# A hybrid of scan, linear attention and ternary feed-forward on one core: the bias behind a one-column copy, weights' sums moved, a shifted instruction stream and a third output bank

## The chip, the cores and the metric

The kernel runs on one core of a Trainium2 chip. The core has engines that each work through their own list of instructions in turn: PE (TensorE, matrix products, with PEld for its weight loads), DVE (VectorE), ACT (ScalarE), POOL (GpSimd), and SP (SyncE), which issues most transfers. They wait for one another through semaphores. The metric is the device time of one execution in microseconds (us). Before the change it is 1060.16 us, the median of three runs (1059.4 to 1060.26). One execution was also recorded by the hardware profiler; all views of the profile are of that one.

## The reference

The input x has two sequences of 2048 rows with 256 columns. Four layers are added to it, each on the layer-normalised x: a gated scan, a feed-forward with ternary weights, a higher-order linear attention, and the same feed-forward again.

```python
x = x + _L0_attn_a_ref(_layernorm(x), gamma, w_qkva)      # q * scan(sigmoid(a), kv) of an RMS-normed x
x = x + _L0_ffn_ref(_layernorm(x), W1, b1, W2, b2)
x = x + _L0_attn_b_ref(_layernorm(x), W_q, W_k, W_v, W_o)
x = x + _L0_ffn_ref(_layernorm(x), W1, b1, W2, b2)
...
# feed-forward
h = jnp.einsum('bsd,fd->bsf', x, _ternary(W1)) + b1       # 1024 hidden columns
h = jax.nn.gelu(h, approximate=False)
out = jnp.einsum('bsf,df->bsd', h, _ternary(W2)) + b2
...
# attention: 16 heads of 64, states S_K, C_QV, G carried from row to row
k_C = jnp.einsum('bhk,bhkv->bhv', k_t, C_QV)
G = G + k_t[..., :, None] * k_C[..., None, :]
S_K = S_K + k_t[..., :, None] * k_t[..., None, :]
C_QV = C_QV + q_t[..., :, None] * v_t[..., None, :]
o_t = jnp.einsum('bhk,bhkv->bhv', q_t, jnp.einsum('bhkj,bhjv->bhkv', S_K, C_QV) - G)
```

`_ternary(W)` rounds W over the mean of its magnitudes to -1, 0 or 1.

## The kernel before

All of x stays in SBUF (`x_sb`), as 32 chunks of 128 rows. Four chunks are a block; the list `blocks` has eight, those of the two sequences in turn. The work has three stages, each in a scope of its own: the **front** (scan and first feed-forward, 0 to 227 us), **attention** (227 to about 945 us) and the **last feed-forward** (to the end). In each scope the order of the instructions on PE, DVE, ACT and POOL is written out by hand: an engine runs its instructions in the order in which the Python code emits them. SP's transfers are issued in their order too.

**Front** (`front`). It starts with units of the scan (`s_` statistics, `r_` normalised rows, `t_` turned rows, `q_` the scan itself, `a_` the sum into x) and then loops over the eight blocks. For block i it emits `ffn_in` (eight steps, one for each 128 hidden columns: four matmuls into one bank `ph`, one GELU on ACT; after every second step `Hidden.split` makes a high half `hh` on ACT and the rest `hl` on DVE) and `ffn_out` (eight steps of eight matmuls into two banks `o`, then DVE adds them to x). For i = 0 to 3 the scan of a later unit runs between the steps of `ffn_in` (`scan_steps`, whose products can be cut into m parts of the 512 columns). The rows of the feed-forward to come are prepared by `fs_` (statistics: bn_stats on DVE, four small operations on POOL that give `rs` and `nb`), `fq_` (normalised rows `xn` on ACT, squares turned by DVE, out to DRAM and back by SP) and `fe_` (`halves_end`: the conversion `xh` on ACT, the rest `xl` on DVE). `ffn_bias(g0)` (L548 to L551) adds b2 to a whole block of x on POOL; it must come before DVE's sum of that block. Here it stands at the end of the loop's body, for the block after.

**The seam.** Attention multiplies by Strassen's scheme with seven products (`Seven`), so it needs sums of the weights' quarters. `weights_kv(w, t)` (L465 to L472) makes them with four POOL operations of 128 x 512. Here `later` has three of them, for wk, wv and wq, emitted at i = 4, 5 and 6. Attention's first pair of chunks (one of each sequence) is prepared by `then`: `attention_stats` (four small POOL operations at the end), `attention_rows` (`xn` on ACT, squares, SP's round trip) and `attention_turned` (the copy `xnT_first`). They stand after step 4 of `ffn_in` of i = 6, in `ffn_out` of i = 6, and after `ffn_in` of i = 7.

**Attention** (`attention`). At first `pair_sums(0)` makes the four sums `S` of the first pair on POOL, `norm_stats` the statistics of pair 1 (DVE, then POOL), and the products of k, q and v of pair 0 follow, with `norm_rows` of pair 1 on ACT in the middle. `Seven.go(i)` emits product i of seven on PE and its eviction or sum: 1, 5, 6 and 4 are copied by ACT, 0, 7 and 3 added by DVE; the banks X and Z of k and of v are the same two (ring `oT`). The tables `in_two` and `first_in_two` say which products are cut into two matmul calls (the second one for pair 0 alone). Then the loop over 32 steps s (`NS`, one chunk each): `inter`, `products`, `intra`, `evict`, `update`, `outward`, and transfers through DRAM that turn keys and units (`keys_out`, `units_out`, `turn_rows`, `turn_end`). In its last four steps the class `Last` starts the last feed-forward's block 0: it brings the ternary weights back from DRAM in four transfers each, issued by ACT (`weights`, `part`: `w1r_back` from s = 28, `w2r_back` from s = 29, the latter with `part(4)`), and fills PE with steps of `ffn_in`.

**Last feed-forward.** For each block: `ffn_in`, from step 4 on the statistics of block i + 3, `halves_end` of block i + 2, rows and squares of block i + 3, `ffn_out` with the store, and then `ffn_bias` of block i + 1. In the last block `ffn_out` (L523 to L546) runs all eight steps for chunks 0 to 2 and then all eight for chunk 3, whose sum goes into the second half of the bank that holds chunk 2.

Of the kernel before, what the change touches and what calls it, by code (L numbers as in the profile page):

```python
# [23 lines left out]
P = 128  # L24
# [20 lines left out]
def kernel(  # L45
# [477 lines left out]
    def ffn_out(g0, hid, store=False, tag="ps"):  # L523

        banks = [bank([P, 2, D], f"o{g0}_{i}", tag) for i in range(2)]
        if store and g0 == blocks[-1]:
            order = [(f, range(BC - 1)) for f in range(NF)] + [(f, range(BC - 1, BC)) for f in range(NF)]
        else:
            order = [(f, range(BC)) for f in range(NF)]
        for f, cs in order:  # L530
            for c in cs:
                to = banks[c // 2][:, c % 2, :]
                for k, h in enumerate((hid.hi, hid.lo)):
                    nc.tensor.matmul(  # L534
                        to, lhsT=h[f // 2][:, f % 2, c * P : (c + 1) * P], rhs=w2r[:, f, :],
                        start=(f == 0 and k == 0 and c % 2 == 0), stop=(f == NF - 1 and k == 1),
                        skip_group_check=True,
                    )
                m = 1 if len(cs) < BC and c > 1 else 2
                if f == NF - 1 and (c % 2 == 1 or m == 1):  # L540
                    g = g0 + c + 1 - m
                    xs = x_sb[:, g : g + m, :]
                    nc.vector.tensor_tensor(xs, xs, banks[c // 2][:, c % 2 + 1 - m : c % 2 + 1, :], ALU.add)  # L543
                    if store:
                        nc.sync.dma_start(out=rows(of, g, m), in_=xs)
            yield  # L546

    def ffn_bias(g0):  # L548

        xs = x_sb[:, g0 : g0 + BC, :]  # L550
        nc.gpsimd.tensor_tensor(xs, xs, b2_sb.unsqueeze(1).to_broadcast([P, BC, D]), ALU.add)  # L551

# [7 lines left out]
    def front(scan_pool, ffn_pool, tern_pool, then, later):  # L560
# [112 lines left out]
        for i in range(NB):  # L673
            u, g0 = i + 5, blocks[i]
            more, scans = i + 1 < NB, u < len(units)
            hid, staged = hidden(ffn_pool, g0)
            steps = ffn_in(g0, fn.pop(i), hid, staged)
            if i == 0:
                ffn_bias(g0)
            if scans:  # L680
                ys[u] = []
                products = scan_steps(scan_pool, units[u][0], xnT[u], last[units[u][0] // CPB], ys[u], 2 if i > 1 else 1)
                for j in range(4):
                    run(products, 1)
                    run(steps, 1)
                    if i == 0 and j == 0:
                        a_(4)
                        fq_(1)
                run(products)
                if i == 3:  # L690
                    fq_(5, scan_pool, "xn")
            else:
                run(steps, 4)
                if i == 4:
                    fs_(7)
                if i == NB - 2:
                    then[0]()
            if u + 1 < len(units):
                s_(u + 1)
            if i == 0:  # L700
                fs_(2)
            run(steps)
            if u + 1 < len(units):
                r_(u + 1)
            if i == 5:
                wq = const.tile([P, ND, H * DK], FP, tag="wq", name="wq")
                nc.sync.dma_start(out=wq, in_=w_q.rearrange("(c p) e -> p c e", p=P))
            if not more:
                wo = const.tile([P, NPR, D], FP, tag="wo", name="wo")
                nc.sync.dma_start(out=wo, in_=w_o.rearrange("(c p) e -> p c e", p=P))  # L710
                then[2]()

            steps = ffn_out(g0, hid, tag="out")
            if i > 3 and i - 4 < len(later):
                later[i - 4]()
            if i == 2:
                ffn_weights_away()
            if scans:
                fe_(i + 1)
                run(steps, 2)  # L720
                a_(u)
                run(steps, 3)
                if u + 1 < len(units):
                    t_(u + 1)
            if i < 3:
                fq_(i + 2)
                fs_(i + 3)
                if i == 2:
                    fs_(6)
            elif i == 3:  # L730
                fq_(6)
                fe_(5)
            elif i + 2 < NB:
                fe_(i + 2)
                if i + 3 < NB:
                    fq_(i + 3)
            if i == NB - 2:
                then[1]()
            run(steps)
            if more:  # L740
                ffn_bias(blocks[i + 1])

# [6 lines left out]
    def attention(keep, pool, state, last):  # L751
# [22 lines left out]
            pairs[n] = x, S  # L774

        in_two = {"kN": (1, 5, 3), "vN": (1, 5)}
        first_in_two = {"kN": (2, 4, 6, 7), "vN": ()}

        class Seven:

# [220 lines left out]

        NS = len(steps)
        pair_sums(0)
        stats = norm_stats(norm_pool, pair(1), bias=True)
        k, q, v = Seven(0, "kN", "oT"), Seven(0, "qT", "uT"), Seven(0, "vN", "oT")
        k.go(2, 1, 0, 5)
# [21 lines left out]
        for s in range(NS):  # L1028
# [27 lines left out]
            if s < NS - 2:  # L1056
                last.part()
            elif s == NS - 2:
                last.part(None)
            if s >= 3:  # L1060
                outward(s - 3, 1)
            intra(s, "S", "kN", "p1", "uT")
# [7 lines left out]
            if not more:  # L1070
                if first:
                    units_out(s)
                    turn_rows(s, "uN")
                else:
                    evict(s - 2, "oT", dve)
                last.begin(first)
                fill = last.fill
                fill(1)
                if first:
                    fill(1)  # L1080
                    last.his()
                    evict(s - 2, "oT", act)
                else:
                    units(s)
                    fill(2)
                    last.his()
            elif first:
                if s != 2:
                    k = Seven(n + 1, "kN", "uT" if s > 0 else "oT")
                    k.go(2)  # L1090
                k.go(1)
                if s >= 2:
                    evict(s - 2, "oT")
                else:
                    units_out(s)
                    turn_rows(s, "uN")
                k.go(0, 5)
                if s == 0:
                    k.go(6)
            else:  # L1100
                if s >= 2:
                    evict(s - 2, "oT", dve)
                if s > 1 or not more:
                    units_end(s - 1)
                units_out(s)
                turn_rows(s, "uN")
                if n + 2 < CPB:
                    raw = norm_squares(pool, pair(n + 2), [xn], 2, "xraw", 1)
                if s > 1:
                    q.go(2)  # L1110
                    v.go(2)
                for part in (q, v) if s > 1 else (v, q):
                    part.go(1)
                if s == NS - 3:
                    last.part()
                q.go(0, 5)
                v.go(0, 5)
                if s == 1:
                    units_end(s - 1)
                q.go(6)  # L1120
                v.go(6)
# [60 lines left out]
            if s == NS - 3:  # L1182
                last.part(None)
                last.weights(False)
                last.part(4)
            if s >= 2:
                outward(s - 2, 0)
        last.out()
# [24 lines left out]
    def pair(n):  # L1213
        return [b * CPB + n for b in range(B)]
# [116 lines left out]
    with (  # L1331
        tc.tile_pool(name="scan", bufs=2) as scan_pool,
        tc.tile_pool(name="ffn1", bufs=2) as ffn_pool,
        tc.tile_pool(name="tern", bufs=2) as tern_pool,
        tc.manual_schedule(engines=by_hand),
    ):

        warm = bank([P, P], "warm")
        for _ in range(12):
            nc.tensor.matmul(warm, lhsT=ones, rhs=ones, start=True, stop=True)  # L1340
        nc.scalar.activation(table, ones[:, :1], AF.Sigmoid)
        front(
            scan_pool, ffn_pool, tern_pool, (attention_stats, attention_rows, attention_turned),
            [lambda: weights_kv(wk, wk_t), lambda: weights_kv(wv, wv_t), lambda: weights_kv(wq, wq_t)],
        )
    front_ctx.close()

# [1 line left out]
    with tc.tile_pool(name="keep", bufs=3) as keep_pool:  # L1349
# [10 lines left out]
        with tc.tile_pool(name="ffn2", bufs=1) as ffn_pool, tc.manual_schedule(engines=by_hand):  # L1360
            two_rings()
            steps, rhs, raws = last.outs, last.turns, {}
            for i, g0 in enumerate(blocks):
                more, ahead = i + 1 < len(blocks), i + 3 < len(blocks)
                if i > 0:
# [6 lines left out]
                    steps = ffn_out(g0, hid, True, "out")  # L1372
                    if i + 2 < len(blocks):
                        rhs[i + 2] = halves_end(raws.pop(i + 2), rows_room(ffn_pool, blocks[i + 2], bufs=2))
                if ahead:
                    if i > 0:
                        last.rows(blocks[i + 3])
                    raws[i + 3] = norm_squares(ffn_pool, chunks(blocks[i + 3]), last.xn, 1)
                run(steps)
                if more:  # L1380
                    ffn_bias(blocks[i + 1])


# [35 lines left out]
```

## Time and profile before

| what | us |
|---|---|
| three runs | 1059.4, 1060.26, 1060.16 |
| profiled execution | 1059.29 |
| its span, first to last instruction | 1057.1 |
| PE busy | 1046.6 |
| DVE, ACT, POOL busy | 732.1, 613.3, 185.2 |
| `ffn_out` of the front's last block | 219.7 to 227.2 |
| POOL's `S` of pair 0 | 227.5 to 229.3 |
| PE's last matmul | 1053.62 |

In a timeline a row has start, time, engine, line, operation, the tiles written and read, the shape and the count; in brackets stands the idle time of the engine before it and what ended that. In the list of waits a row says who waited for whom: us in total, times, the longest. "issue" is idle time that no engine ended. PE's matmuls overlap, so a group's time runs to the modelled end of its last one; the time between the starts of two groups is the better measure. The span is shorter than the time of the execution by 2.2 us.

### The profile page before, as it was taken

The numbers are of one execution on the slowest core, as the hardware profiler recorded it, in microseconds if no ns is written. First come the engines' busy times: TensorE is split into PE (matmuls) and PEld (weight loads), VectorE is DVE, ScalarE is ACT, GpSimd is POOL, SyncE is SP. The second block draws the span as 40 slices with busy tenths as digits, with TensorE's granted clock in tenths as the row PEclk, the third lists the DMA queues.
The fourth block names the chain that finished last, engine by engine and source line by source line (L and its number), as shares of the span: only waits on it lengthen the run. The fifth ranks groups of instructions, "written<-read, shape, count | busy, mean of one in ns | idle before, by whom it ended". The sixth has DMA issues, their size and how long they took to land.

```text
span 1057.1 us, 43926 instructions
## 1 busy us (share of the span) xinstructions
PE 1046.6 (99%) x20136; PEld 847.1 (80%) x20136; DVE 732.1 (69%) x1047; ACT 613.3 (58%) x813; POOL 185.2 (18%) x282
## 2 busy tenths in 40 slices
PE   9999999999999999999999999999999999999998
PEld 7567889887778887878778788787877877888987
DVE  7987788846675765766666666666675766668973
ACT  4567779754645555445554455545545554668884
POOL 3433243831101001011010110101101010014230
PEclk9999999999999999999999999999999999999999
DMA  9231112203432433423324243242332435123321
GB/s 313 81 120 41 41 41 80 80 28 114 143 124 90 133 102 105 142 81 124 121 85 143 86 139 111 75 142 103 122 122 83 141 105 170 35 101 101 120 81 40
DMA packets 80826, 111.24 MB, mean 105 GB/s; under 512 B 8321, under 2 KB 66561, under 8 KB 80385
## 3 DMA queue, kind: packets, MB, share of 16 engines
q1 hardware_dynamic: 79024, 106.07, 30.3%
q8 instruction: 157, 2.57, 1.0%
q10 hardware_dynamic: 1584, 2.36, 0.8%
q14 instruction: 29, 0.23, 0.1%
q0 software_dynamic: 32, 0.00, 0.0%
HBM read 57.81 MB, written 50.59 MB: 103 GB/s over the span
## 4 chain that ended last, share of the span: by engine, by line
PE 87%; DVE 5%; DMA 2%; ACT 2%; issue 2%; POOL 1%; SPq 0%; ACTq 0%; DVEq 0%; POOLq 0%
PE hy L962 10%; PE o L534 7%; PE h L512 7%; PE hkN_X L827 6%; PE hp L882 6%; PE hqT_X L819 6%; PE hvN_X L827 6%; PE pq L368 4%; PE pq L390 3%; PE huT L899 3%; PE hoT L899 3%; PE huT L913 3%; PE hS L939 3%; PE hoT L913 3%; PE hM L939 3%; PE hqT_Z L819 3%
## 5 line engine op out<-in xcount | busy, mean ns | idle before, releaser
L888 DVE TENSOR_TENSOR p<-hp,mask 128x512 f32<-128x512 f32 x128 | 82.3, 684 | 83.4 <-PE hp L882 83.4
L962 PE MATMUL hy<-wo,oT 128*128 128x256 f32 x512 | 124.0, 386 | 0.0
L962 PEld LDWEIGHTS hy<-wo,oT 128*128 128x128 f32 x512 | 93.5, 190 | 19.1 <-issue 6.9
L773 POOL TENSOR_TENSOR S<-xnT 128x128 f32<-128x128 f32 x30 | 13.9, 463 | 514.8 <-ACT xnT L312 514.8
L497 DVE TENSOR_TENSOR hl<-h,hh 128x1024 fp32r<-128x1024 f32 x60 | 83.0, 1395 | 28.3 <-ACT hh L491 28.1
L518 ACT ACTIVATE h<-h,b_sb 128x512 f32<-128x512 f32 x120 | 77.6, 682 | 42.9 <-PE h L512 33.7
L924 ACT COPY uT<-huT 128x512 f32<-128x512 f32 x32 | 18.7, 585 | 123.3 <-PE huT L913 123.3
L194 ACT ACTIVATE xn<-x_sb,nb,rs 128x256 f32<-128x256 f32 x124 | 65.2, 592 | 18.3 <-POOL nb L180 18.3
L951 DVE TENSOR_TENSOR S<-S,hS 128x512 f32<-128x512 f32 x60 | 41.3, 688 | 42.3 <-PE hS L939 39.3
L259 DVE STREAM_TRANSPOSE squN<-uT 128x1024 f32<-128x1024 f32 x31 | 63.8, 2058 | 5.5 <-ACT uT L926 5.1
L259 DVE STREAM_TRANSPOSE sqkT<-kN 128x1024 f32<-128x1024 f32 x32 | 65.8, 2058 | 1.3 <-ACT kN L859 1.2
L981 ACT COPY kT<-rawkT 128x1024 f32<-128x1024 f32 x32 | 66.7, 2085 | 0.0
L981 ACT COPY uN<-rawuN 128x1024 f32<-128x1024 f32 x31 | 64.7, 2086 | 3.2 <-DMA w2r_back<-dw2r 2.9
L491 ACT CAST hh<-h 128x1024 fp32r<-128x1024 f32 x60 | 63.1, 1051 | 1.9
L534 PE MATMUL o<-w2r,hl 128*128 128x256 f32 x256 | 61.1, 281 | 0.4 <-DVE hl L497 0.2
L534 PE MATMUL o<-w2r_back,hh 128*128 128x256 f32 x248 | 60.6, 284 | 0.9 <-DVE x_sb L543 0.9
L534 PE MATMUL o<-w2r_back,hl 128*128 128x256 f32 x248 | 60.6, 283 | 0.9 <-DVE hl L497 0.7
L534 PE MATMUL o<-w2r,hh 128*128 128x256 f32 x256 | 61.3, 282 | 0.0
L859 ACT COPY vN<-hvN_X 128x512 f32<-128x512 f32 x16 | 9.4, 586 | 78.8 <-PE hvN_X L827 78.8
L162 DVE BATCH_NORM_STATS2 st<-x_sb 128x6 f32<-128x256 f32 x128 | 51.3, 401 | 2.3 <-DMA x_sb<-in_x_dram 2.3
L833 DVE TENSOR_TENSOR kN<-kN,hkN_Y 128x512 f32<-128x512 f32 x16 | 11.0, 688 | 60.2 <-ACT kN L842 60.2
L534 PEld LDWEIGHTS o<-w2r,hl 128*128 128x128 f32 x256 | 48.2, 188 | 1.5 <-DVE hl L497 1.0
(227 smaller groups left out, 2583.0 us busy)
## 6 DMA issues: line engine op xcount, KB each, us to landing
dsqkT<-sqkT SPq DMA_DIRECT2D x32, 512.0 KB, 3.8
rawkT<-dsqkT SPq DMA_DIRECT2D x128, 128.0 KB, 2.9
dsquN<-squN SPq DMA_DIRECT2D x31, 512.0 KB, 3.2
rawuN<-dsquN SPq DMA_DIRECT2D x124, 128.0 KB, 3.0
dsqxn<-sqxn SPq DMA_DIRECT2D x14, 512.0 KB, 2.7
rawxn<-dsqxn SPq DMA_DIRECT2D x56, 128.0 KB, 2.9
out_dram<-x_sb SPq DMA_DIRECT2D x15, 256.0 KB, 3.0
x_sb<-in_x_dram SPq DMA_DIRECT2D x7, 512.0 KB, 9.0
```

What stands on the lines that cost most here:

```text
L194: nc.scalar.activation(xn[:, c, :], x_sb[:, g, :], AF.Identity, bias=nb[:, c : c + 1], scale=rs[:, c : c + 1],)
L259: nc.vector.transpose(to, src)
L497: nc.vector.tensor_tensor(self.lo[a], h, self.hi[a], ALU.subtract)
L512: nc.tensor.matmul(ph, lhsT=w1r[:, d, f * P : (f + 1) * P], rhs=r[:, d, :], start=(d == 0 and k == 0), stop=(d == ND - 1 and k == 1),)
L518: nc.scalar.activation(h[:, f % 2, :], ph, AF.Gelu, bias=b1_sb[:, f : f + 1])
L534: nc.tensor.matmul(to, lhsT=h[f // 2][:, f % 2, c * P : (c + 1) * P], rhs=w2r[:, f, :], start=(f == 0 and k == 0 and c % 2 == 0), stop=(f ...
L819: nc.tensor.matmul(to[:, j, :], lhsT=self.B[i][:, j * P : (j + 1) * P], rhs=self.A[i], start=(new and j == 0), stop=True, skip_group_check ...
L827: nc.tensor.matmul(to[:, cols], lhsT=self.A[i], rhs=self.B[i][:, cols], start=(new and j == 0), stop=True, skip_group_check=True,)
L882: nc.tensor.matmul(banks[h][halves[c], p, :], lhsT=d[s][left][halves[h], p, halves[c]], rhs=d[s]["qT"][halves[h], p, halves[c]], start=Tru ...
L888: nc.vector.tensor_tensor(d[s][nm][:, h], banks[h], mask8, ALU.mult)
L962: nc.tensor.matmul(py, lhsT=d[s]["oT"][:, p, :], rhs=wo[:, p, :], start=(p == 0), stop=(p == NPR - 1),)
L981: act(t, d[s]["r" + nm].rearrange("p t q -> p q t"))
```

## The change

- **Bias.** `ffn_bias` begins with a copy of one column of `b2_sb` onto itself on DVE. POOL's bias reads that column, so it can't start until DVE, in its order, has come to the copy. The calls move: in the front from the end of the body to just after `fe_` of the same block (for i = 4 to 6 after the steps named in the diff), in the last feed-forward to just after `halves_end`.
- **Order of the front.** `fe_(5)` goes from i = 3 to i = 4, `fe_(6)` stays at i = 4, `fe_(7)` goes from i = 5 to i = 6; `fs_(7)` and `fq_(7)` go from i = 4 to i = 5. `later` is `weights_kv(wk)` alone, at i = 6 after the bias; `attention_stats` follows it there; `attention_rows` stands after step 2 of `ffn_in` of i = 7. `weights_kv` of wq and wv go into attention, between `pair_sums(0)` and the statistics of pair 1.
- **Instruction stream.** The scan's products at i = 1 are cut in two (`2 if i > 0`), and the products 2, 4 and 6 of v of pair 0 too. Each cut adds a matmul call; a call with 32-bit operands is two weight loads and two matmuls in the trace.
- **Weight back.** `part(4)` becomes `part(2)`; at s = 30 one part is issued where before all that was left would have been, and one more after the eviction and the outgoing squares of that step.
- **Last bank.** Chunk 3 of the last block sums into a third bank of the ring `ps`, with `start` on its first matmul.

```diff
--- before.py
+++ after.py
@@ -525,28 +525,31 @@
         banks = [bank([P, 2, D], f"o{g0}_{i}", tag) for i in range(2)]
         if store and g0 == blocks[-1]:
             order = [(f, range(BC - 1)) for f in range(NF)] + [(f, range(BC - 1, BC)) for f in range(NF)]
+            banks.append(bank([P, 2, D], f"o{g0}_2"))
         else:
             order = [(f, range(BC)) for f in range(NF)]
         for f, cs in order:
             for c in cs:
-                to = banks[c // 2][:, c % 2, :]
+                at = c // 2 if len(cs) > 1 else 2
+                to = banks[at][:, c % 2, :]
                 for k, h in enumerate((hid.hi, hid.lo)):
                     nc.tensor.matmul(
                         to, lhsT=h[f // 2][:, f % 2, c * P : (c + 1) * P], rhs=w2r[:, f, :],
-                        start=(f == 0 and k == 0 and c % 2 == 0), stop=(f == NF - 1 and k == 1),
+                        start=(f == 0 and k == 0 and (c % 2 == 0 or at == 2)), stop=(f == NF - 1 and k == 1),
                         skip_group_check=True,
                     )
                 m = 1 if len(cs) < BC and c > 1 else 2
                 if f == NF - 1 and (c % 2 == 1 or m == 1):
                     g = g0 + c + 1 - m
                     xs = x_sb[:, g : g + m, :]
-                    nc.vector.tensor_tensor(xs, xs, banks[c // 2][:, c % 2 + 1 - m : c % 2 + 1, :], ALU.add)
+                    nc.vector.tensor_tensor(xs, xs, banks[at][:, c % 2 + 1 - m : c % 2 + 1, :], ALU.add)
                     if store:
                         nc.sync.dma_start(out=rows(of, g, m), in_=xs)
             yield
 
     def ffn_bias(g0):
 
+        nc.vector.tensor_copy(b2_sb[:, :1], b2_sb[:, :1])
         xs = x_sb[:, g0 : g0 + BC, :]
         nc.gpsimd.tensor_tensor(xs, xs, b2_sb.unsqueeze(1).to_broadcast([P, BC, D]), ALU.add)
 
@@ -679,7 +682,7 @@
                 ffn_bias(g0)
             if scans:
                 ys[u] = []
-                products = scan_steps(scan_pool, units[u][0], xnT[u], last[units[u][0] // CPB], ys[u], 2 if i > 1 else 1)
+                products = scan_steps(scan_pool, units[u][0], xnT[u], last[units[u][0] // CPB], ys[u], 2 if i > 0 else 1)
                 for j in range(4):
                     run(products, 1)
                     run(steps, 1)
@@ -690,11 +693,12 @@
                 if i == 3:
                     fq_(5, scan_pool, "xn")
             else:
+                if i == 5:
+                    fs_(7)
+                elif not more:
+                    run(steps, 2)
+                    then[1]()
                 run(steps, 4)
-                if i == 4:
-                    fs_(7)
-                if i == NB - 2:
-                    then[0]()
             if u + 1 < len(units):
                 s_(u + 1)
             if i == 0:
@@ -711,12 +715,13 @@
                 then[2]()
 
             steps = ffn_out(g0, hid, tag="out")
-            if i > 3 and i - 4 < len(later):
-                later[i - 4]()
             if i == 2:
                 ffn_weights_away()
+            if i == 4:
+                fe_(5)
             if scans:
                 fe_(i + 1)
+                ffn_bias(blocks[i + 1])
                 run(steps, 2)
                 a_(u)
                 run(steps, 3)
@@ -729,16 +734,18 @@
                     fs_(6)
             elif i == 3:
                 fq_(6)
-                fe_(5)
-            elif i + 2 < NB:
-                fe_(i + 2)
-                if i + 3 < NB:
-                    fq_(i + 3)
-            if i == NB - 2:
-                then[1]()
+            elif i == 4:
+                fe_(6)
+                ffn_bias(blocks[i + 1])
+            elif i == 5:
+                ffn_bias(blocks[i + 1])
+                fq_(7)
+            elif i == 6:
+                fe_(7)
+                ffn_bias(blocks[i + 1])
+                later()
+                then[0]()
             run(steps)
-            if more:
-                ffn_bias(blocks[i + 1])
 
 
 
@@ -774,7 +781,7 @@
             pairs[n] = x, S
 
         in_two = {"kN": (1, 5, 3), "vN": (1, 5)}
-        first_in_two = {"kN": (2, 4, 6, 7), "vN": ()}
+        first_in_two = {"kN": (2, 4, 6, 7), "vN": (2, 4, 6)}
 
         class Seven:
 
@@ -1001,6 +1008,8 @@
 
         NS = len(steps)
         pair_sums(0)
+        weights_kv(wq, wq_t)
+        weights_kv(wv, wv_t)
         stats = norm_stats(norm_pool, pair(1), bias=True)
         k, q, v = Seven(0, "kN", "oT"), Seven(0, "qT", "uT"), Seven(0, "vN", "oT")
         k.go(2, 1, 0, 5)
@@ -1056,7 +1065,7 @@
             if s < NS - 2:
                 last.part()
             elif s == NS - 2:
-                last.part(None)
+                last.part()
             if s >= 3:
                 outward(s - 3, 1)
             intra(s, "S", "kN", "p1", "uT")
@@ -1073,6 +1082,8 @@
                     turn_rows(s, "uN")
                 else:
                     evict(s - 2, "oT", dve)
+                if first:
+                    last.part()
                 last.begin(first)
                 fill = last.fill
                 fill(1)
@@ -1182,7 +1193,7 @@
             if s == NS - 3:
                 last.part(None)
                 last.weights(False)
-                last.part(4)
+                last.part(2)
             if s >= 2:
                 outward(s - 2, 0)
         last.out()
@@ -1341,7 +1352,7 @@
         nc.scalar.activation(table, ones[:, :1], AF.Sigmoid)
         front(
             scan_pool, ffn_pool, tern_pool, (attention_stats, attention_rows, attention_turned),
-            [lambda: weights_kv(wk, wk_t), lambda: weights_kv(wv, wv_t), lambda: weights_kv(wq, wq_t)],
+            lambda: weights_kv(wk, wk_t),
         )
     front_ctx.close()
 
@@ -1372,13 +1383,13 @@
                     steps = ffn_out(g0, hid, True, "out")
                     if i + 2 < len(blocks):
                         rhs[i + 2] = halves_end(raws.pop(i + 2), rows_room(ffn_pool, blocks[i + 2], bufs=2))
+                if more:
+                    ffn_bias(blocks[i + 1])
                 if ahead:
                     if i > 0:
                         last.rows(blocks[i + 3])
                     raws[i + 3] = norm_squares(ffn_pool, chunks(blocks[i + 3]), last.xn, 1)
                 run(steps)
-                if more:
-                    ffn_bias(blocks[i + 1])
 
 
 # ---- launch: one core; inputs and outputs as the reference has them ----
```

## Prediction

> **What bounds the kernel now.** I read the page first, then the waits of the matmul engine (PE), then the timelines of PE, ACT, DVE and POOL where PE stands still.
>
> ```profile
> span 1057.1 us, 43926 instructions
> ...
> PE 1046.6 (99%) x20136; PEld 847.1 (80%) x20136; DVE 732.1 (69%) x1047; ACT 613.3 (58%) x813; POOL 185.2 (18%) x282
> ```
>
> PE is busy from 1.05 to 1053.9 us. A time is won only where PE stands still, and lost wherever an instruction before PE comes late. POOL's 18% says nothing of its order: it works its list strictly in turn, and so does ACT. The two views that decide this case are POOL's and ACT's timelines around the seam between the front and attention:
>
> ```profile
> 209.47 1.29 POOL L469 TENSOR_TENSOR wq_t<-wq 128x512 f32<-128x512 f32 x1
> ...
> 214.59 2.41 POOL L551 TENSOR_TENSOR x_sb<-x_sb,b_sb 128x1024 f32<-128x1024 f32 x1
> 227.50 0.46 POOL L773 TENSOR_TENSOR S<-xnT_first 128x128 f32<-128x128 f32 x1 [10.50 <-PE o L534]
> ...
> 229.41 0.22 POOL L174 TENSOR_SCALAR rs<-mv 128x2 f32<-128x2 f32 x1
> ...
> 230.78 0.23 POOL L180 TENSOR_SCALAR nb<-nb 128x2 f32<-128x2 f32 x1
> ```
> ```profile
> 215.03 1.05 ACT L491 CAST hh<-h 128x1024 fp32r<-128x1024 f32 x1
> ...
> 236.64 1.09 ACT L194 ACTIVATE xn<-x_sb,nb,rs 128x256 f32<-128x256 f32 x2
> 238.09 0.58 ACT L859 COPY kN<-hkN_X 128x512 f32<-128x512 f32 x1 [0.36 <-PE hkN_X L827]
> ```
>
> The reader is to see that S (pair_sums) waits 10.5 us for the last matmul of the front, that pair 1's `rs` and `nb` stand behind it although DVE had their statistics by 207.4, and that ACT's `xn` of pair 1 (236.64) stands ahead of the eviction at 238.09. PE's `hvN_X` begins at 238.78, just after that eviction's end (238.67), in the bank it frees.
>
> PE's own stops, in the places the change touches:
>
> ```profile
> PE o L534 <- DVE x_sb L543: 0.9, 1, 0.9
> PE o L534 <- DVE hl L497: 0.9, 3, 0.4
> PE hoT L913 <- issue: 0.8, 1, 0.8
> ```
> ```profile
> 370.48 1.49 PE L913 MATMUL hoT<-p,vN 64*64 64x64 f32 x64
> ```
> ```profile
> 718.56 1.11 PE L913 MATMUL hoT<-p,vN 64*64 64x64 f32 x64
> ```
>
> The last two are the same 64 matmuls in two rounds: one takes 0.38 us longer, and no engine released it.
>
> **Last bank (gain 1.1).** PE starts a matmul at 1050.51 and the next at 1051.73, where 0.12 is usual: chunk 3 shares its bank with chunk 2, which DVE is still reading. A third bank takes that wait away. The new bank comes from the ring of six whose oldest tile was read long before. The end follows PE, DVE's last add and SP's last store, all 1.1 us earlier.
>
> **Bias held (gain 1.9).** In the last feed-forward the bias (2.41 us) meets DVE's subtractions: two `hl` take 3.49 us at 1011.90 against 1.23 each alone, `xl` 3.56 at 959.54. PE loses 0.23 at 967.6, 0.50 at 972.0 and 0.54 at 1014.3; I take 1.1 of the 1.27, since the statistics stay in front of one `hl`. In the front PE loses 0.36, 0.25 and 0.26 at 177.7, 193.2 and 195.4, where POOL works on weights and bias; I take 0.8. Between 0 and 2.1 in all. The new one-column copy is at most like the 0.17 us of DVE's smallest rows, 16 times, beside 31% idle: nothing.
>
> **The 65 instructions (gain 2.4).** Splitting `pq` at i = 1 and vN's products 2, 4 and 6 adds 15 matmul calls; the time of the halves is that of the whole (216 against 429 to 432 ns from start to start): nothing by itself. But it moves every later instruction in PE's instruction stream. The page has 157 instruction packets of 16 KB on queue 8: 256 instructions each. Counting PE's instructions, the stops in `hoT` are all at the same place modulo 256, so they are waits for the next packet. One round of attention is nine packets long, and the stop comes back in nine rounds with 0.16 to 0.33 us, 2.4 us in sum. The packet that is late left at 368.92, behind the 512 KB of `dsqkT` that ran from 367.0 to 368.8. Moved by 65 instructions it is asked for about 0.47 us earlier, at some 366.8, 0.2 us ahead of that burst. The other eight packets of a round keep their distances. So I take all 2.4; 0 if the margin of 0.2 fails, and 2.4 lost if another packet falls into a burst.
>
> **Weight back in three parts (gain 1.2).** At 886.0 to 889.4 ACT issues four parts in a row, and PE then loses 0.82 at 893.9 to a late instruction packet, and 1.5 more in five smaller stops from 866 to 908. With two parts there and two in the next step the transfers are shorter by half at that point, and all packets shift by 65. I take about half of the 2.3, from 0 to 2.
>
> **Front's order: the first loss (6.5).** `fe_`, `fq_` and `fs_` move by one block; for blocks 5 and 6 the halves are ready with ffn_in's need to within 0.1 us (two conversions of 2.35 on ACT, then 2.27 on DVE): nothing. The point is block 6. There POOL gets, in this order: the bias of block 7, held until `xl` of block 7 is done; weights_kv(wk); the four operations of attention_stats. On the clock of before: ACT ends the last `hh` of block 6 at 207.88, converts `xh` (2.25) to 210.15, DVE's `xl` (2.27) ends 212.4. Bias 2.41: 214.9. The four weights operations are 5.12 (209.47 to 214.59) plus one meeting with DVE's `hl` (1.2): 221.2. Then 1.6 (229.41 to 231.0): `nb` at 222.8. ACT now has attention_rows after two steps of ffn_in(7), so it asks for `nb` at 216.1 and stands 6.7 us, with the GELUs of steps 2 to 7 queued behind it. PE finishes ffn_in from free banks at 219.7, uses the first two steps' hidden until 221.8 and waits. ACT: `xn` 1.1, two GELUs 1.25, `hh` 1.05 to 226.2; DVE's `hl` to 227.4. PE has stood 5.6 us, then follows ACT's 2.25 us for each 1.87 of its own: ffn_out ends at 233.7 instead of 227.2. Between 5.1 (no meeting with DVE) and 7.5 (a second one). SP's round trip of the first rows (7.7 us from `xn` to landing in this trace) ends at 231.7, inside that. The wo load behind it on SP is needed 50 us later.
>
> **Attention's start: the second loss (4.2).** After S (end 229.3) POOL now does weights_kv(wq) and (wv), 8 x 1.28 = 10.2 us, then the 1.6 us for pair 1: `nb` at 241.2 instead of 231.0. ACT stands at 236.6 until then, `xn` 1.1, the kN eviction 0.58: 242.95. PE's `hvN_X` starts at 243.0 instead of 238.78. wq_t and wv_t themselves are in time (230.7 for a use at 234.2; 235.8 for 240.6). Bounds 3.9 to 4.5.
>
> **PE's clock (1.75).** No row has PE idle for 5 us in the middle. At the end the granted clock falls to 0.50 by 1055.9, 2.0 us after the last matmul; at the start 24 warm-up matmuls are 213 ns apart instead of 109 for about 3.5 us. So each of the two idles may cost up to 1.75 us, or nothing: 0 to 3.5. I take one of the two. The Trainium skill, "TensorE: Matmul & The Clock Gate", Part 1, would have it that one idle window of about 3.4 us must pass whole, in a free-running grid; by that the longer idle halves the clock more often than the shorter, an estimate of 1.5 us in place of 1.75. The row asks for less idleness than the page.
>
> **Sum.** Gains 1.1 + 1.9 + 2.4 + 1.2 = 6.6; losses 6.5 + 4.2 + 1.75 = 12.45; +5.9. The profiled execution took 1059.29 us (span 1057.1 and 2.2 around it), so 1065.2; the median of before, 1060.16, lies 0.9 above it, so 1066.0. This case's own range: losses 9.0 to 15.5 against gains 7.5 to 3.5, that is 1061.5 to 1072.
>
> **Rivals.** (1) Faster: both `nb` are ready when ACT asks (216.1 and 236.6), because the small operations get past the weights on POOL. Then only the gains stay: 1053.6. It decides from the point where the two waits sum to less than 6.6 us. Against it stands the row of 229.41, which waited 22 us behind S. (2) The bias isn't held: the copy waits for nothing that matters. Then POOL is done with block 6 before ACT asks, the first loss and the 1.9 of the hold go, and 1.1 + 2.4 + 1.2 against 4.2 and 0.9 of clock leave 1060.5. DVE's rows are in turn everywhere, which speaks against. (3) The new place of the packets is no better: instead of 2.4 + 1.2 won, 2.4 lost: 1072. The burst is only 0.2 us away, but the nine rounds agree to 0.03.
>
> **Chances.** Forecast 0.60; rival 1 0.22; rival 2 0.10; rival 3 0.08. A change under 0.2% (2.1 us) can hardly be told from none. Faster: 0.22 and half of rival 2, 0.27; same 0.06; slower 0.67. The range takes in rival 1 and nearly rival 3: 1053.5 to 1071.5.
>
> **What will show it.** First loss: ACT's `xn` of pair 0 idle some 6 us before it with POOL's `nb` named, PE's `o` of block 7 stopped. Second: ACT's `xn` of pair 1 near its predecessor plus 4 us, PE stopped before `hvN_X`. Gains: `hoT` at 1.11 in every round, no 0.9 us wait in the last block, `xl` at 2.3 throughout. I am wrong if ACT doesn't wait for either `nb`.

## The result, and the profile after

The changed kernel takes 1066.89 us (median of six runs, 1066.52 to 1069.37) against 1059.38 us for the kernel before (six runs, 1058.19 to 1060.26). The ratio is 1.0077, with a 95% interval of 1.0065 to 1.009: about 7.5 to 8 us slower. The profiled execution took 1066.52 us, the one of before 1059.29.

Where the time went is read from PE's starts: the same matmul is looked up in both traces, and the differences are taken from place to place.

| stretch | after - before, us |
|---|---|
| front, to the first product of `ffn_out` of block 7 | -1.22 |
| `ffn_out` of block 7, to the first product of attention | +7.32 |
| from there to `hvN_X` | +3.97 |
| from there to the first `hy` of chunk 0 | +1.61 |
| loop, chunk 3 to chunk 26 | -3.36 |
| end of the loop, chunk 26 to chunk 29 | +2.34 |
| last feed-forward, to `ffn_out` of block 7 | -2.09 |
| last bank | -1.22 |

The sum is +7.35. The page's first lines:

```profile
span 1064.8 us, 44002 instructions
...
PE 1045.1 (98%) x20166; PEld 853.6 (80%) x20166; DVE 718.4 (67%) x1063; ACT 612.2 (57%) x813; POOL 180.1 (17%) x282
```

PE's busy time is 1.5 us less than before and the span 7.7 us longer: it is PE's idle time that grew. The list of PE's waits (us, times, the longest) names the places:

```profile
PE o L536 <- ACT hh L491: 4.4, 1, 4.4
PE hvN_X L834 <- ACT kN L866: 3.8, 1, 3.8
PE hS L946 <- issue: 1.4, 1, 1.4
PE hoT L920 <- issue: 1.0, 1, 1.0
PE o L536 <- DVE hl L497: 0.7, 1, 0.7
PE hp L889 <- issue: 0.6, 1, 0.6
```

The first, second and fifth are the seam. POOL's and ACT's timelines show what stands behind them:

```profile
211.19 2.41 POOL L554 TENSOR_TENSOR x_sb<-x_sb,b_sb 128x1024 f32<-128x1024 f32 x1 [14.78 <-issue]
213.55 1.30 POOL L469 TENSOR_TENSOR wk_t<-wk 128x512 f32<-128x512 f32 x1
214.93 2.36 POOL L470 TENSOR_TENSOR wk_t<-wk,wk_t 128x512 f32<-128x512 f32 x1
...
221.26 0.24 POOL L180 TENSOR_SCALAR nb<-nb 128x2 f32<-128x2 f32 x1
233.61 0.46 POOL L780 TENSOR_TENSOR S<-xnT_first 128x128 f32<-128x128 f32 x1 [12.11 <-PE o L536]
...
244.24 1.26 POOL L472 TENSOR_TENSOR wv_t<-wv,wv_t 128x512 f32<-128x512 f32 x1
...
246.97 0.23 POOL L180 TENSOR_SCALAR nb<-nb 128x2 f32<-128x2 f32 x1
```
```profile
221.54 1.09 ACT L194 ACTIVATE xn<-x_sb,nb,rs 128x256 f32<-128x256 f32 x2 [6.66 <-POOL nb L180]
...
247.24 1.09 ACT L194 ACTIVATE xn<-x_sb,nb,rs 128x256 f32<-128x256 f32 x2 [4.39 <-POOL nb L180]
248.23 0.56 ACT L866 COPY kN<-hkN_X 128x512 f32<-128x512 f32 x1
```

Twice ACT stands before `xn` for a POOL operation of 0.24 us that has 6 or 10 us of weights in front of it, and both times PE stands a little later (4.35 us from 220.55, 3.78 us from 245.07). With each, PE's clock is halved: from 222.70 and from 250.01. In the windows the third number from the end is the granted clock:

```profile
223.00:225.00 2.00, 0.10 (x1) 0.10 (x1) 0.88 (x2) 1.97 (x4) 0.00 (x0) 0.50 0.18 72
225.00:227.00 2.00, 1.32 (x5) 1.03 (x6) 1.10 (x1) 1.97 (x4) 0.00 (x0) 0.50 0.20 72
227.00:230.00 3.00, 3.00 (x17) 3.00 (x17) 1.86 (x2) 2.84 (x5) 0.00 (x0) 0.58 0.28 79
...
250.00:252.00 2.00, 2.00 (x10) 1.91 (x10) 1.81 (x3) 0.59 (x1) 0.00 (x0) 0.50 0.14 57
```

In the loop the 64 products that took 1.49 us at 370.48 before now take:

```profile
382.16 1.11 PE L920 MATMUL hoT<-p,vN 64*64 64x64 f32 x64
```

In the last feed-forward the `xl` that the prediction names (DVE, 959.54 before) is short again, the line of before and then the one of after:

```profile
959.54 3.56 DVE L203 TENSOR_TENSOR xl<-rawxn,xh 128x1024 fp32r<-128x1024 f32 x1 [2.32 <-ACT xh L202]
```
```profile
969.08 2.23 DVE L203 TENSOR_TENSOR xl<-rawxn,xh 128x1024 fp32r<-128x1024 f32 x1 [1.64 <-ACT xh L202]
```

At the end of the loop, where I had expected gains, PE's timeline has new stops that no engine ended:

```profile
903.40 0.92 PE L920 MATMUL hoT<-p,vN 64*64 64x64 f32 x46 [0.97 <-issue]
909.15 0.91 PE L946 MATMUL hS<-kN 64*64 64x64 f32 x23 [1.40 <-issue]
913.49 0.68 PE L889 MATMUL hp<-qT,uT 64*64 64x64 f32 x28 [0.62 <-issue]
```

### The profile page after: what moved, and what is told of

Its sections match the earlier page's. It is cut to its first block, busy times and chain, and to the rows that moved or that the text cites. A ratio compares the mean times of both kernels' runs of the same rounds, so it can differ in the third digit from the quotient of the medians.

```text
span 1064.8 us, 44002 instructions
## 1 busy us (share of the span) xinstructions
PE 1045.1 (98%) x20166; PEld 853.6 (80%) x20166; DVE 718.4 (67%) x1063; ACT 612.2 (57%) x813; POOL 180.1 (17%) x282
## 4 chain that ended last, share of the span: by engine, by line
PE 81%; POOL 3%; ACT 1%; issue 1%; DVE 1%; ACTq 0%; POOLq 0%; DVEq 0%
PE hy L969 11%; PE o L536 9%; PE h L512 8%; PE hp L889 6%; PE hvN_X L834 6%; PE hkN_X L834 5%; PE hqT_X L826 5%; PE hS L946 3%; PE hoT L906 3%; PE huT L920 3%; PE huT L906 3%; PE hoT L920 3%; PE hM L946 3%; PE hqT_Z L826 3%; PE hvN_Z L834 3%; PE hkN_Z L834 2%
## 5 line engine op out<-in xcount | busy, mean ns | idle before, releaser
L497 DVE TENSOR_TENSOR hl<-h,hh 128x1024 fp32r<-128x1024 f32 x60 | 73.0, 1220 | 38.9 <-ACT hh L491 38.6
L554 POOL TENSOR_TENSOR x_sb<-x_sb,b_sb 128x1024 f32<-128x1024 f32 x16 | 38.8, 2424 | 155.3 <-DVE b_sb L552 80.5
L536 PEld LDWEIGHTS o<-w2r,hh 128*128 128x128 f32 x256 | 49.3, 192 | 4.9 <-ACT hh L491 4.6
```

The lines of the kernel that those rows point to most:

```text
L497: nc.vector.tensor_tensor(self.lo[a], h, self.hi[a], ALU.subtract)
L536: nc.tensor.matmul(to, lhsT=h[f // 2][:, f % 2, c * P : (c + 1) * P], rhs=w2r[:, f, :], start=(f == 0 and k == 0 and (c % 2 == 0 or at == ...
```

## Experiments

My theory: the two places of POOL's order, with the clock behind them, make the whole loss. The rivals: PE is held there by something else; and, for the last stops, either the three parts or the shift is at fault. The kernels ran in three groups, each beside the kernel before: medians 1058.7, 1059.71 and 1058.9 us. Ratios to those compare groups; by the ratio of 1.0077 the changed kernel stands at 1066.85 in the first. A stretch or a row is read from the one profiled execution of a kernel, a time is the median of several, so the two need not agree to a microsecond.

**Statistics of pair 0 ahead of wk's sums.**

```diff
-                later()
                 then[0]()
+                later()
```

> The changed kernel with attention_stats ahead of weights_kv(wk) in the front's block 6; wq and wv stay in front of pair 1's statistics. My theory: POOL's order at block 6 costs two things, PE's stops of 4.4 and 0.7 us in the last ffn_out and the half clock after them (together 6.5 to 7.3 us), so the time falls from 1066.9 to about 1060.0, ACT's xn of pair 0 shows no wait for nb, and the row hvN_X is still stopped by about 3.8 us. Rival: ffn_out is held by the pace of GELU, hh and hl at that place anyway, or the wait only moves to wk's sums, which now come 1.6 us later; then no more than 3 us is won: 1064 or above.

Measured: 1062.08 us, ratio 1.0033 (1.002 to 1.0046). In ACT's timeline `xn` of pair 0 comes at 216.25 instead of 221.54:

```profile
216.25 1.09 ACT L194 ACTIVATE xn<-x_sb,nb,rs 128x256 f32<-128x256 f32 x2 [1.39 <-POOL nb L180]
...
241.20 1.09 ACT L194 ACTIVATE xn<-x_sb,nb,rs 128x256 f32<-128x256 f32 x2 [4.41 <-POOL nb L180]
```

The 4.35 us stop and the half clock with it are gone; from `ffn_out` of block 7 to attention it is +1.28 instead of +7.32, with ACT still waiting 1.39 us for `nb`. So 6.0 us of the loss are the order of two neighbours in POOL's list. The median fell by only 4.8 us, 2 short of what I expected. The profiled execution, at 1064.59 us the longest of the ten, lies only 1.9 below that of the changed kernel, and shows where such a difference can go: the second stop stayed, its stretch of half clock was longer here (+2.77 instead of +1.61), and the end of the loop lost +4.53 instead of +2.34, with half clock there too.

**Sums of wq ahead of S, those of wv behind the statistics of pair 1.**

```diff
+        weights_kv(wq, wq_t)
         pair_sums(0)
-        weights_kv(wq, wq_t)
-        weights_kv(wv, wv_t)
         stats = norm_stats(norm_pool, pair(1), bias=True)
+        weights_kv(wv, wv_t)
```

> The changed kernel with wq's four sums in front of pair_sums(0) (POOL stands still there for 12 us) and wv's four behind pair 1's statistics. My theory: pair 1's nb is ready before ACT asks for it, PE's stop of 3.8 us before hvN_X goes and with it about 1.6 us of half clock: 1066.9 less 5.0 to 5.5, about 1061.7. The first stop (4.4 us) stays. Rival: the sums of wv, now 1.6 us later, become the wait of v.go, or S is late behind wq; then 2 us or less are won: 1065 or above.

Measured: 1062.5 us, ratio 1.0029 (1.0016 to 1.0042). In ACT's timeline the wait is gone:

```profile
243.71 1.09 ACT L194 ACTIVATE xn<-x_sb,nb,rs 128x256 f32<-128x256 f32 x2
245.18 0.59 ACT L866 COPY kN<-hkN_X 128x512 f32<-128x512 f32 x1 [0.38 <-PE hkN_X L834]
```

`hvN_X` comes +0.02 after what precedes it instead of +3.97, and the stretch behind it is -0.08 instead of +1.61. With the stop the clock's loss went too. The sums of wv, ended at 243.2, held nobody up.

**Both orders.** The first edit, with wq's sums behind wk's in the front and wv's behind the statistics of pair 1.

```diff
-                later()
                 then[0]()
+                later()
...
-        weights_kv(wq, wq_t)
-        weights_kv(wv, wv_t)
         stats = norm_stats(norm_pool, pair(1), bias=True)
+        weights_kv(wv, wv_t)
...
-            lambda: weights_kv(wk, wk_t),
+            lambda: (weights_kv(wk, wk_t), weights_kv(wq, wq_t)),
```

> Both at once: nb of pair 0, then wk and wq in the front's block 6, S and nb of pair 1 in front of wv. If the two waits and their two stretches of half clock are the whole loss, the gains of the other parts stay: 1066.9 - 6.9 - 5.2 = 1054.8, some 4.5 us faster than the kernel before. If something else is lost too (POOL, with ten operations of 128x512 in a row before S, makes S late by DVE's meetings), S begins later than the last product of ffn_out plus 0.5 us and the time is 1057 or above.

Measured: 1056.85 us, ratio 0.9981 (0.997 to 0.9992), now faster than before, 2 us short of what I expected. Neither of the two long stops is left. But ACT still waits 1.39 us for `nb` of pair 0, as with the first edit alone, and S is late behind wq's sums, two of which take over 2 us beside DVE's operations. POOL's timeline:

```profile
222.35 2.28 POOL L469 TENSOR_TENSOR wq_t<-wq 128x512 f32<-128x512 f32 x1
...
229.29 0.46 POOL L780 TENSOR_TENSOR S<-xnT_first 128x128 f32<-128x128 f32 x1
...
232.58 0.23 POOL L180 TENSOR_SCALAR nb<-nb 128x2 f32<-128x2 f32 x1
```

The seam keeps +1.58 up to attention's first product, 1.28 of it as with the first edit alone, and +0.58 behind it, where PE waits 0.28 us for S. The end of the loop loses 4.48, with this stop in it (PE's timeline):

```profile
900.01 0.91 PE L946 MATMUL hS<-kN 64*64 64x64 f32 x22 [2.16 <-issue]
```

**Weights back as before, alone.**

```diff
             elif s == NS - 2:
-                last.part()
+                last.part(None)
...
-                if first:
-                    last.part()
                 last.begin(first)
...
-                last.part(2)
+                last.part(4)
```

> The changed kernel with the ternary weights brought back as in the kernel before (part(4), then all that is left), the 65 instructions kept. Between 900 and 915 us the changed kernel lost 2.3 us to stops of PE that no engine released. Theory A, the three parts put the transfers where the instruction packets are late: the stops go or shrink to those of before, 1064.6. Theory B, the shift by 65 put the packets where the transfers are: the stops stay, 1066.9 within 0.5, or it gets worse by up to 1.2.

Measured: 1068.3 us, ratio 1.009 (1.0062 to 1.0117), no faster than the changed kernel. In its profile, taken from the shortest of its runs (1064.95 us), the end of the loop loses 0.84 instead of 2.34. Theory A has the one trace, theory B the median; this run leaves it open.

**The changed kernel again, then without the cut products, then without cut products and three parts.**

```diff
-..., ys[u], 2 if i > 0 else 1)
+..., ys[u], 2 if i > 1 else 1)
...
-        first_in_two = {"kN": (2, 4, 6, 7), "vN": (2, 4, 6)}
+        first_in_two = {"kN": (2, 4, 6, 7), "vN": ()}
```

The third has the edit of the weights as well.

> The changed kernel itself, unaltered, beside the next three on the same chip, so that terms of 1 to 3 us can be told: 1066.9 within 1.0.

> The changed kernel without the 65 instructions (products at i = 1 and v's 2, 4 and 6 whole again), the three parts kept. In the loop the hoT stops of 0.26 to 0.42 us come back in nine rounds, 3.3 us. For the stretch 885 to 920: theory A (the three parts put the transfers of the weights where the packet is fetched) has the 2.3 us stay: 1070.2. Theory B (the shift moved the packets there) has them go: 1067.9. If neither alone does it, it takes both: also 1067.9, and the next kernel tells.

> The changed kernel with neither the 65 instructions nor the three parts: bias, order of the front and last bank alone. Loop as in the kernel before (+3.3), tail as in the kernel before (-2.3): 1067.9 by either theory; if the tail's loss is due to the changed seam, for example because the transfers' phase is another, it stays: 1070.2.

Measured: 1068.61 (ratio 1.008, 1.0061 to 1.0099), 1066.68 (1.007, 1.0045 to 1.0095) and 1066.13 us (1.0058, 1.0039 to 1.0077). The first lies 0.7 above what I had allowed, beside a kernel before that was higher too; its ratio is the old one. The loss at the end of the loop is +2.32 in the first, -0.09 and +0.03 in the others: it goes with the shift, whether the parts are three or not (theory B). But I had expected 3.3 us of stops to come back in the loop, and they didn't. In PE's timeline, at the place of the 1.49 us row, stands without any cut product:

```profile
384.40 1.17 PE L920 MATMUL hoT<-p,vN 64*64 64x64 f32 x64
```

The trace says why the cut products aren't needed. Of the 65 instructions by which attention moved, 60 are loads and products of the 15 cuts, and 5 are separate semaphore instructions that PE has anyway in the changed front (118 in the trace against 113). So this kernel is still shifted by 5.

**The kernel before, with 4 and with 60 instructions more.** The first cuts product 2 of v of pair 0, the second makes all the cuts of the change; nothing else.

```diff
-        first_in_two = {"kN": (2, 4, 6, 7), "vN": ()}
+        first_in_two = {"kN": (2, 4, 6, 7), "vN": (2,)}
```

> The kernel before with one product of v of pair 0 (number 2) cut in two, four more instructions on PE and nothing else. Theory C: the late packet of the loop is at the very edge, and a shift by four or five instructions is enough; then nine rounds gain 0.26 to 0.4 us each, 1059.4 - 3.3 = 1056.1, with the tail within 1 us. Theory D: the stops went in the changed kernel for another reason (another phase of the transfers), and the place has to move by more than four: hoT stops in nine rounds as before, 1059.4 within 0.7.

> The kernel before with all the cut products, 60 more instructions on PE, nothing else. By what the changed kernel showed, the loop's stops go (-3.3) and the tail gets a second late packet (+0.8 to +2.3): 1057 to 1058.4, that is 1 to 2.4 us faster than before. If the tail's loss belongs to the three parts alone, 1056.1.

Measured: 1056.89 us, ratio 0.999 (0.9976 to 1.0003), and 1058.35, ratio 0.9994 (0.9981 to 1.0007). With 4 instructions eight of the nine stops are gone and the loop gains 3.01 us; in PE's timeline one row with 0.38 us less and the one that stayed:

```profile
370.67 1.11 PE L913 MATMUL hoT<-p,vN 64*64 64x64 f32 x64
...
456.96 1.46 PE L913 MATMUL hoT<-p,vN 64*64 64x64 f32 x64
```

By the medians this kernel is 2 us faster, but the interval just takes in no change. With 60 the loop gains 3.36 and the end of the loop loses 4.62 (in an execution of 1060.14 us, the second longest of ten), most of it in this row of PE's timeline and in the half clock from 892.4 to 899.2:

```profile
892.94 1.54 PE L913 MATMUL hoT<-p,vN 64*64 64x64 f32 x43 [2.90 <-issue]
```

So the shift alone, without three parts and with the seam of before, pays and charges about the same: by the medians the kernel can't be told from the one before.

**Both orders with the weights back as before, and with the cut products undone.**

The edits are those shown above, put together: that of both orders with that of the weights, and that of both orders with this one:

```diff
-..., ys[u], 2 if i > 0 else 1)
+..., ys[u], 2 if i > 1 else 1)
...
-        first_in_two = {"kN": (2, 4, 6, 7), "vN": (2, 4, 6)}
+        first_in_two = {"kN": (2, 4, 6, 7), "vN": ()}
```

> both_orders with the ternary weights brought back as in the kernel before, the 65 instructions kept. If the three parts cause the two stops of 1.14 and 2.38 us at 893 and 900 us and the clock of 0.91 there, 3 to 3.7 us go: 1053.2 to 1054. If the stops only move to other packets, the time stays within 1 us of both_orders: 1056 to 1057.

> both_orders without the cut products (60 of the 65 instructions), the weights back in three parts kept. In shift_undone the loop's gain stayed (nine steps of -0.26 to -0.40) and the tail's loss went. If both hold here, the 4.5 us between rounds 26 and 29 of both_orders go: 1056.9 - 4.5 = 1052.4. If the loop's stops need a certain distance from the old place, which is now smaller, up to 3.3 us come back: 1055.7.

Measured: 1056.31 us, ratio 0.9967 (0.9954 to 0.9981), and 1055.85, ratio 0.9964 (0.9946 to 0.9982). Both beat both kernels, by 3 to 4 us against before; which of the two is better can't be told. In the first the end of the loop still loses 2.18. In the second it loses 0.58, but now the shift is only 3 instructions and two of the nine stops are back (some 0.37 us each), like this one in PE's timeline:

```profile
414.44 1.47 PE L920 MATMUL hoT<-p,vN 64*64 64x64 f32 x64
```

It also lost 1.46 us around 951 to 957, in waits of `o` for `hl` that the changed kernel doesn't have. Its trace leads back to SP's transfer of squares `dsqxn`: 4.75 us from issue to landing (933.29 to 938.04) against 2.7 to 3.6 in the other profiled kernels, so that ACT's conversion `xh_last` waits 1.70 us for the rows and the hidden columns behind it come late. Why that transfer was slow no run shows.

All kernels by their shift, in us against the trace of before:

| shift | kernel | loop | its end |
|---|---|---|---|
| 3 | both orders, shift undone | -2.62 | +0.58 |
| 4 | before plus 4 | -3.01 | -0.43 |
| 5 | shift undone; with parts undone | -3.22; -3.19 | -0.09; +0.03 |
| 60 | before plus 60 | -3.36 | +4.62 |
| 63 | both orders; wq before S; both with weights as before | -3.34; -3.33; -3.33 | +4.48; +2.63; +2.18 |
| 65 | changed, twice; statistics first; weights as before; no hold | -3.36, -3.33; -3.36; -3.37; -3.35 | +2.34, +2.32; +4.53; +0.84; +1.59 |

**The hold taken away.**

```diff
     def ffn_bias(g0):
 
-        nc.vector.tensor_copy(b2_sb[:, :1], b2_sb[:, :1])
```

> The changed kernel without the copy of one column before each bias, so that POOL's bias runs as early as it can; nothing else is altered. It is my second rival made real: POOL is done with bias and wk before the statistics of pair 0 are there, nb comes at about 214.0, PE's stop in ffn_out and the clock after it go (-7.3), and the meetings of bias and DVE come back in the front (+1.4) and the last feed-forward (+2.1): about 1062.7. If the order of POOL's list alone makes the first loss, the bias's time doesn't matter, and the 7.3 us stay: 1068 to 1070.

Measured: 1062.03 us, ratio 1.0033 (1.0019 to 1.0048), as my second rival had the mechanism. POOL, with the same list, is done with bias and wk long before the statistics. Its timeline:

```profile
194.65 2.57 POOL L553 TENSOR_TENSOR x_sb<-x_sb,b_sb 128x1024 f32<-128x1024 f32 x1 [0.78 <-ACT xn L194]
...
201.06 2.28 POOL L472 TENSOR_TENSOR wk_t<-wk,wk_t 128x512 f32<-128x512 f32 x1
213.35 0.23 POOL L174 TENSOR_SCALAR rs<-mv 128x2 f32<-128x2 f32 x1 [10.01 <-DVE mv L163]
```

The stretch to attention is 0.00 instead of +7.32. In return the front gains 0.44 instead of 1.22 and the last feed-forward loses 0.32 instead of winning 2.09. By these two executions the hold alone is worth some 3 us (0.78 and 2.41), and in this order it costs 7.

## Why the prediction was right, and where not

I forecast 1066.0 us (1053.5 to 1071.5) and it is 1066.89. The mechanism of the loss stands; several terms of the sum were wrong and cancelled. That the time is met so closely is in part luck: the forecast change was +5.9 us and the measured one is 7.5, but I started from a median of before that lies 0.8 us above the one measured beside the changed kernel.

| term | forecast | profiled execution |
|---|---|---|
| front's order, first loss | 6.5 | 7.32 with its clock |
| attention's start, second loss | 4.2 | 3.97 |
| PE's clock | 1.75 | 1.61 at the second stop alone |
| bias held | -1.9 | -0.78 and -2.41 (against the run without the hold) |
| 65 instructions | -2.4 | -3.36, and +2.34 at the end |
| three parts | -1.2 | can't be told |
| last bank | -1.1 | -1.22 |

- **First loss.** Read off POOL's list, `nb` was to be there at 222.8 and ACT to ask at 216.1, on the clock of before. In the changed trace, which is 1.22 us ahead at that point, they are 221.50 and 214.88, that is 222.72 and 216.10. Of 5.6 us of PE's stop 4.35 and 0.68 came; the rest passed at half clock, without a further wait of PE. Two experiments remove this loss by different means, by POOL's order (all but 1.28 us) and by an earlier bias (all of it).
- **Second loss.** Right to 0.25 us, and it goes with the order of wv and the statistics.
- **Clock.** I counted one of the two stops. Both brought half clock, and in all eight profiled executions with either of these stops it was so. The second stop's stretch cost 1.61 and 1.62 us where the clock was halved for 3.41 us, 2.49, 2.76, 2.77, 2.88 and 2.88 where it was for 6.83, and -0.08 to -0.10 in the four with the change's front but without this stop. So my bound of 1.75 for one stop was too low as well.
- **Bias held.** The gains were larger than the single stops that I had added up (3.2 against 1.9): in the last feed-forward all `xl` are back at 2.1 to 2.2 us. Of the front's 1.22 us, 0.44 come without the hold. What I had right is that the same hold makes the first loss; rival 2 (1060.5) names the lever, and the run without the hold gave 1062.03.
- **65 instructions.** The late packet behind `dsqkT` was the right reading, but its price was too low: the nine rows of before lie 0.26 to 0.42 us above 1.11, 3.3 in sum, where I had added idle times of 0.16 to 0.33. And the step "moved by 65" was wrong twice. The edge is so sharp that 4 or 5 instructions do nearly the same. And "the other eight packets keep their distances" holds for the rounds of the loop, not for its end, where other transfers run: with a shift of 60 or more every profiled kernel lost 0.84 to 4.62 us there, with 5 or less at most 0.58. In the packet records of the changed trace, PE passes its index 193 (modulo 256) at 897.17 and the next packet leaves only at 901.13, after the transfers of 895.6 to 901.0; in the loop most packets leave 0.5 to 1.0 us after that point. It and the next two land at 902.09, 907.87 and 912.06, and the three stops of PE end 1.3 to 1.4 us behind that, at 903.40, 909.15 and 913.49. I had named this case as "2.4 lost if another packet falls into a burst" and gave it 0.08.
- **Three parts.** Not even the term's sign is shown. Without the shift there is 0.1 us between three parts and the old way (-0.09 and +0.03). With it the old way lost less at the end of the loop in both pairs of profiled executions (0.84 against 2.34, 2.18 against 4.48), but the kernel before with 60 more instructions lost 4.62 without any change of the parts, and of the two ratios one rose (1.0077 to 1.009) and one fell (0.9981 to 0.9967).
- **Last bank.** -1.20 to -1.22 in every kernel that has it, 0.0 in the two that don't.

Not tried: a shift that suits the loop and its end, and both orders without the hold in the front but with it in the last feed-forward.

## What to carry to other kernels

An engine with 17% busy time can set the end when its list is in turn: before a long operation is moved, look for the small one behind it that someone else waits for, and when they ask. A wait added to one instruction delays everything that is queued behind it; the hold was worth 3 us by itself and cost 7 by what stood after it. A gain that comes from where instructions fall in the stream must be checked over the whole kernel, since every later stage is moved with it, and with the smallest shift first.

## What the runs showed of the hardware

- The clock was halved after quite short stops of PE. Stops of 1.95 us (statistics first, at 904) and 2.16 us (both orders, at 898) were followed by it, one of 1.72 us (no hold, at 897) and one of 1.40 us (changed kernel, at 908) were not. It can come after PE has resumed: in the changed kernel PE worked again from 248.85, and the clock fell at 250.0. The halved stretches are 3.4 us long (both orders 900.9 to 904.3) or 6.8 us (before plus 60).
- What counts looks like the idle time within fixed stretches of 3.41 us. Two falls of the clock within one execution lie whole multiples of 3.413 us apart (222.70 and 250.01 in the changed kernel: eight of them). In the 3.41 us before each of the 16 falls ahead of the kernels' ends PE stood idle for 1.95 us or more; of the stretches on that grid that passed at full clock and were not followed by a fall, the emptiest had 1.81 us idle (weights back as before, 219.1 to 222.5). The clock came back after 3.41 us in the five cases in which PE stood idle for at most 0.38 us of them, and after 6.83 us in the eleven with 0.52 us or more.
- The Trainium skill, "TensorE: Matmul & The Clock Gate", Part 1, asks for at least one idle window of about 3.4 us; stops of 1.95 and 2.16 us are too short to hold one, so here the measurement decides. The lengths of the halved stretches, 3.4 and 6.8 us, do agree with one and two of its windows.
- PE's instruction stream comes in packets of 256 instructions: 157 packets before for 40,385 loads, products and semaphore instructions, 158 after for 40,450. Where the packet left only behind a transfer of 512 KB, PE's row was 0.26 to 0.42 us longer in the loop; at the end, where more transfers meet, stops were up to 2.9 us long.
